# A four-layer graph network on one core: bias rows and degrees in fewer products, edge visits among the first weight products, the general path as a branch's body, and the last rows in halves

## The chip, the core and the metric

The kernel runs on one core of one Trainium2 chip. The metric is the device time of one execution in microseconds; the time before is the median of three runs. The engines are named as in the profile: PE (matrix products), PEld (PE's weight loads), DVE, ACT, POOL, and SP, which here only issues transfers and waits.

## The reference, cut to what matters

The inputs are 512 nodes with 512 features (float32) and 16384 edges, sorted by `dst`. Four layers follow one another, each with a residual around it:

```python
edge_index = jnp.stack([src, dst])
h = jnp.maximum(_layernorm(x, axis=-1), 0.0)
x = x + _L0_gnn_ref(h, edge_weight, L0_gnn_W_gcn, L0_gnn_b_gcn, L0_gnn_W_mlp, L0_gnn_b_mlp, edge_index)
h = jnp.maximum(_layernorm(x, axis=-1), 0.0)
x = x + _L1_gnn_ref(...)   # four blocks of sparse attention with a conditioned norm, and an MLP
h = jnp.maximum(_layernorm(x, axis=-1), 0.0)
x = x + _L2_gnn_ref(...)   # three diffusion steps over the symmetric adjacency
h = jnp.maximum(_layernorm(x, axis=-1), 0.0)
x = x + _L3_gnn_ref(...)   # two relational layers with gates; weights are sums of 30 bases
```

The change touches mostly the first layer:

```python
A = zeros((512, 512)).at[edge_index[0], edge_index[1]].add(edge_weights)
deg = jnp.sum(A, axis=1)
dinv = jnp.where(deg > 0, deg ** (-0.5), 0.0)
A_norm = dinv[:, None] * A * dinv[None, :]
for l in range(2):
    h = A_norm @ h
    h = h @ W_gcn[l] + b_gcn[l]
    h = leaky_relu(h @ W_mlp[l] + b_mlp[l], 0.01)
```

## The kernel before, in words

One function, `network`, writes out the whole program in the order in which each engine is to run it. No scheduler reorders it. It is called twice: once with `general=False`, for edge lists whose sorted destinations lie within a spread of ranks, and once with `general=True` inside a branch that is taken only when a flag says that the list was unusual. With these inputs it isn't taken.

**Start.** The edges are read as 128 rows ("chunks") of 128 edges: destinations, sources and types as integers (`e_i`), weights as floats (`e_r`). They are cast, and four PE transposes with one eviction put an edge on each partition (`e_c`, L342 to L345). DVE splits the weights into three bfloat16 parts (`vals`), ACT spreads destinations (`widen_dst`, L354) and values (`widen_vals`, L357) for later one-hot products. PE transposes the second graph weight (`wg2_turned`), so that the product of the two second weights, `W2`, can be formed (`W2_rows`: four rows of four products through `job`, L372). In the kernel before, the first row of `W2` is computed ahead of all visits.

**Edge visits.** `visits(c)` adds chunk c to the counts: DVE makes a one-hot matrix of the sources (`s_hot`, L564, twelve buffers), and for each window of 32 destinations that the chunk can touch a stack of weighted one-hots (`hot_dst`: `oh` L528, `st` L530, for up to sixteen chunks at a time). PE multiplies the two (L572) into one of four PSUM banks (`win`), bfloat16 with 512 columns, 195 products in all. When a window is done, ACT evicts it (`finish`, L549) and a transfer moves its counts to `CP`; after four windows `weigh` (L555) adds the three weight parts with four products of 32 columns each into `AT`.

Between visits, `after` and `spread` hang other work at given chunks, in program order: the other `W2` rows, the first layer norm (`first_moments`, `first_start`, `first_end`, `first_norm`), its transposes (`hT_chunk`), the first weights' products `uT` (`u_job`) and `t0` (`t_job`), and the small conditioning network (`cond_sine`, `cond_first`, `cond_silu`, `cond_second`). `job` takes a PSUM bank from the pool `mm`, which has two.

**After the last visit.** `decode(0)` splits the counts of the first 128 destinations on DVE (L609 to L613). The degrees come from four products with an all-ones matrix (`deg_ps`, through `calls`, L99), the fourth of them after `weigh(3)` and the last job `t_job(3)`. DVE takes the diagonal (L635), `neg_rsqrt` gives `dinv`, and `AT` is scaled by it. Then two bias rows, `b_gcn[l] @ W_mlp[l]`, are formed by `row_job`: four products each with the bias broadcast over 128 columns (L372). `decode(1)` and `decode(2)` follow on DVE, and then the four node products with the normalised adjacency (L675, L677), with `decode(3)` after the first.

**The rest.** Attention blocks, diffusion and the relational layers follow. The sums over bases (`more`, L216 on DVE, fed by POOL's transfers) are put between the other steps throughout. In the last layer each 128-row chunk of the output is one product of 4 float32 and 24 bfloat16 parts into one bank, an addition on DVE (L1203) and one transfer (L1204). After the network, every engine loads the flag (L1221) and goes through the branch (L1222), whose empty side comes first and the general network second; the end of the program is at L1245.

Of the kernel before, what the change touches and what calls it, by code (L numbers as in the profile page):

```python
# [9 lines left out]
F32 = mybir.dt.float32  # L10
# [57 lines left out]
def network(ctx, tc, a, out, flag_i, general):  # L68


    nc = tc.nc

    const = ctx.enter_context(tc.tile_pool(name="const", bufs=1))
# [176 lines left out]
    with ExitStack() as pe:  # L250
# [6 lines left out]
        e_i = edges.tile([P, 3, P], I32, name="e_i")  # L257
        e_r = edges.tile([P, 4, P], F32, name="e_r")
        nc.sync.dma_start(e_i[:, 0, :], a["dst"].rearrange("(c e) -> c e", e=P))
        nc.scalar.dma_start(e_i[:, 1, :], a["src"].rearrange("(c e) -> c e", e=P))  # L260
        nc.sync.dma_start(e_i[:, 2, :], a["edge_type_2"].rearrange("(c e) -> c e", e=P))
        nc.scalar.dma_start(e_r[:, 3, :], a["edge_weight"].rearrange("(c e) -> c e", e=P))
        wg1, wm2, wm1, wg2 = (weights.tile([P, K, D], F32, name="w") for _ in range(4))
# [76 lines left out]

        for i in range(3):
            nc.vector.tensor_copy(e_r[:, i, :], e_i[:, i, :])  # L342
        e_c = edges.tile([P, 4, EC], F32, name="e_c")
        transposed(e_c, [e_r[:, i, :] for i in range(4)], nc.vector.tensor_copy)
        dst, src, kind, wt = (e_c[:, i, :] for i in range(4))  # L345
# [156 lines left out]

        spread(0, 1, [f for c in range(1, K) for f in W2_rows(c)])
        for c in range(K):
            after(5 + c, first_moments, c)
            after(11 + c, first_norm, c)
            after(15 + c, hT_chunk, c)
        after(8, first_start)
        after(10, first_end)
        spread(20, 2, [f for j in range(K) for f in u_job(j)])  # L510
# [41 lines left out]
        def weigh(k):  # L552
# [3 lines left out]
            nc.scalar.copy(AT[:, k, :], ps)  # L556

        def visits(c):
            for i, p in enumerate(PIECES):
                if p[3] <= c < p[4] and (i, c // 16) not in groups:  # L560
                    groups[i, c // 16] = (max(p[3], c // 16 * 16),
                                          hot_dst(p, max(p[3], c // 16 * 16), min(p[4], c // 16 * 16 + 16)))
            s = hot.tile([P, N], BF16, name="s_hot")
            nc.vector.tensor_scalar(s, node_ids, src[:, c : c + 1], None, op0=OP.is_equal)  # L564
            for i, p in enumerate(PIECES):
                w = p[2]
                if not p[3] <= c < p[4]:
                    continue
                if w not in banks:
                    banks[w] = win.tile([P, N], F32, name="win")  # L570
                g0, st = groups[i, c // 16]
                nc.tensor.matmul(banks[w], st[:, c - g0, :, :], s, start=(left[w] == total[w]), stop=(left[w] == 1))  # L572
# [50 lines left out]

        decode(0)
        deg_ps = win.tile([P, N], F32, name="win")
        calls(deg_ps, [(all_ones, AT[:, k, :]) for k in range(3)], last=False)
        if not general:
            weigh(3)
        t3 = []
        for call in t_job(3, t3.append):  # L630
            call()
        calls(deg_ps, [(all_ones, AT[:, 3, :])], first=False)
        deg = small.tile([P, K], F32, name="deg", bufs=1)
        for c in range(K):
            nc.vector.scalar_tensor_tensor(e_r[:, c, :], deg_ps[:, chunk(c)], 1.0, ident, op0=OP.mult, op1=OP.mult,  # L635
                                           accum_out=deg[:, c : c + 1])
# [3 lines left out]
        nc.scalar.copy(t0[:, 3, :], t3[0])  # L640
        n = neg_rsqrt(least, 0.0, [P, K],
                      lambda: nc.vector.tensor_scalar(has_deg, deg, 0.0, -1.0, op0=OP.is_gt, op1=OP.mult))
        nc.vector.tensor_mul(dinv, n, has_deg)
# [244 lines left out]
    with ExitStack() as ph:  # L888
# [55 lines left out]
        for i in range(NB):  # L944
# [189 lines left out]
    for l in range(2):  # L1134
# [56 lines left out]
        for c in range(K):  # L1191
            ps = product([(hT[:, k, chunk(c)], root[:, k, :]) for k in range(K)]
                         + [(t[:, k, chunk(c)], part[:, k, :])
                            for k in range(K) for t, parts in ((C0T, u[0]), (C1T, u[1])) for part in parts])
            if l == 0:
# [9 lines left out]
        hT = nT  # L1205
        wr = wrel[1] if l == 0 else None

@with_exitstack
def kernel(ctx: ExitStack, tc: tile.TileContext, a: dict, out: bass.AP):
    nc = tc.nc
    ctx.enter_context(nc.allow_non_contiguous_dma(reason="biases with a feature per partition"))

    ctx.enter_context(tc.manual_schedule())
    flag_i = ctx.enter_context(tc.tile_pool(name="flag", bufs=1)).tile([1, 1], I32, name="flag_i")
    with ExitStack() as body:
        network(body, tc, a, out, flag_i, general=False)

    missed = nc.values_load(flag_i[:1, :1], min_val=0, max_val=1)  # L1221
    with tc.If(missed < 1) as none:  # L1222
        pass
    with none.Else(), ExitStack() as body:
        network(body, tc, a, out, flag_i, general=True)
# [23 lines left out]
```

## Time and profile before

| | |
|---|---|
| median of 3 runs | 851.45 us (850.77 to 851.7) |
| profiled execution | 852.14 us, of which span 850.4 us |
| PE busy | 817.5 us, 96% of the span |
| DVE busy | 676.5 us, 80% |
| ACT, POOL busy | 321.0 us, 64.2 us |
| DMA | 128.41 MB, mean 151 GB/s |
| first product of `W2` starts | 10.13 us |
| first product of `uT` starts | 33.54 us |
| last visit ends, degree products begin | 102.29 us |
| scaled `AT` meets `t0`, first product | 117.06 us |
| last addition on DVE (L1203) | 839.97 to 840.66 us |
| last issue of the output's transfer | 840.69 to 841.02 us |

All stretches of time are measured from the start of the span. Matrix products are pipelined: the interval between the starts of two is what PE is held by one, while its listed duration is longer. A float32 product of 512 columns is two instructions in the trace. A group of lines such as "PE ps L372 x8" in the chain of waits is eight such instructions, or four products.

### The profile page before, as it was taken

How to read it: one execution, taken by the hardware profiler on the slowest of the kernel's cores; microseconds unless marked ns; L12 is line 12 of the kernel's file. 1: busy time of each engine (PE TensorE's matmuls, PEld its weight loads, DVE VectorE, ACT ScalarE, POOL GpSimd, SP SyncE). 2: the span in 40 equal slices, each digit the busy share in tenths (PEclk: the TensorE clock that was granted, in tenths of full speed). 3: DMA queues.
4: the chain of work that ended last, by engine and by line, in shares of the span. 5: the costliest groups of instructions: out<-in, count | busy, mean ns of one | idle time of the engine just before them, and what ended most of it. 6: DMA issues, size and time to landing. Idle time of an engine off the chain costs nothing.

```text
span 850.4 us, 8126 instructions
## 1 busy us (share of the span) xinstructions
PE 817.5 (96%) x2549; PEld 394.1 (46%) x2549; DVE 676.5 (80%) x1183; ACT 321.0 (38%) x647; POOL 64.2 (8%) x135
## 2 busy tenths in 40 slices
PE   7999999999999999999999999999999999999995
PEld 4434344455444644444744445644446544444442
DVE  7777867878888999888997788998888967788620
ACT  4453413432654433563424752324653122311400
POOL 7000010000001001000101010101010100010000
PEclk9999999999999999999999999999999999999998
DMA  9200146213569365478457586545688720141000
GB/s 232 64 6 17 42 148 247 99 63 112 155 175 323 117 215 204 120 225 275 162 168 291 147 256 215 186 146 161 186 296 329 239 90 3 74 146 53 1 25 28
DMA packets 50693, 128.41 MB, mean 151 GB/s; under 512 B 6992, under 2 KB 7536, under 8 KB 49616
## 3 DMA queue, kind: packets, MB, share of 16 engines
q0 software_dynamic: 17552, 66.83, 24.3%
q1 hardware_dynamic: 32800, 60.84, 23.0%
q8 instruction: 22, 0.36, 0.2%
q14 instruction: 31, 0.25, 0.1%
q10 hardware_dynamic: 288, 0.13, 0.1%
HBM read 108.90 MB, written 6.29 MB: 135 GB/s over the span
## 4 chain that ended last, share of the span: by engine, by line
PE 56%; DVE 20%; DMA 7%; SPq 6%; ACT 5%; issue 4%; DVEq 0%; ACTq 0%
PE ps L99 25%; DVE wrel L216 8%; PE sp L99 7%; DMA pT<-turned 6%; SPq L933 6%; PE ps L372 5%; PE ps L1035 5%; PE win L572 5%; PE tr L119 3%; PE sp L804 2%; DVE st L156 2%; PE sp L909 2%; PE sp L666 1%; ACT p L915 1%; DVE z L1025 1%
## 5 line engine op out<-in xcount | busy, mean ns | idle before, releaser
L216 DVE SCALAR_TENSOR_TENSOR wrel<-basis,att,wrel 128x2048 f32<-128x2048 f32 x116 | 264.9, 2341 | 0.0
L99 PE MATMUL ps<-w,oT 128*128 128x512 f32 x288 | 129.5, 595 | 1.0 <-DVE x L1108 1.0
L99 PE MATMUL ps<-yT,w 128*128 128x512 f32 x256 | 112.9, 594 | 0.0
L99 PE MATMUL ps<-w,yT 128*128 128x512 f32 x224 | 101.1, 595 | 1.2 <-ACT yT L126 0.7
L200 POOL DMA_DIRECT2D basis<-in_L_gnn_basis_dram x60 | 45.2, 754 | 694.5 <-DVE wrel L216 530.2
L99 PEld LDWEIGHTS ps<-w,oT 128*128 128x128 f32 x288 | 53.1, 190 | 65.0 <-issue 56.4
L99 PEld LDWEIGHTS ps<-yT,w 128*128 128x128 f32 x256 | 48.2, 190 | 61.9 <-issue 60.9
L99 PEld LDWEIGHTS ps<-w,yT 128*128 128x128 f32 x224 | 41.1, 190 | 48.0 <-issue 44.9
L1035 PE MATMUL ps<-yT,w 128*128 128x256 f32 x256 | 58.4, 382 | 2.9 <-ACT yT L120 2.9
L131 ACT ACTIVATE g<-mv,eps_t 128x1 f32<-128x1 f32 (+1 forms) x45 | 13.3, 295 | 126.2 <-DVE mv L158 126.2
L915 ACT ACTIVATE p<-ns,stat 128x512 f32<-128x512 f32 x64 | 45.5, 711 | 35.7 <-DVE stat L913 35.6
L909 PE MATMUL sp<-kT,qT 128*128 128x512 f32 x128 | 57.6, 593 | 1.1 <-ACT kT L893 1.1
L1035 PEld LDWEIGHTS ps<-yT,w 128*128 128x128 f32 x256 | 47.4, 190 | 14.3 <-ACT yT L120 6.2
L572 PE MATMUL win<-s_hot,st 128*128 128x512 bf16 x195 | 50.4, 379 | 0.5 <-DVE s_hot L564 0.5
L913 DVE CUSTOM_DVE_ANT_0 ns<-sp,lnC 128x512 f32<-128x512 f32 x64 | 43.2, 688 | 5.5 <-PE sp L909 5.5
L905 ACT ACTIVATE p<-p,stat 128x512 f32<-128x512 f32 x64 | 43.7, 707 | 0.0
L564 DVE TENSOR_SCALAR s_hot<-node_ids,e_c 128x512 bf16<-128x512 f16 x128 | 39.9, 359 | 4.1 <-PE win L572 3.6
L909 PEld LDWEIGHTS sp<-kT,qT 128*128 128x128 f32 x128 | 24.2, 190 | 32.1 <-issue 29.9
L572 PEld LDWEIGHTS <-st 128*128 128x128 bf16 x195 | 18.7, 98 | 37.1 <-issue 23.4
L668 ACT ACTIVATE mod<-sp 128x512 f32<-128x512 f32 x64 | 32.9, 597 | 5.5 <-PE sp L666 5.5
L902 DVE RECIPROCAL stat<-stat 128x1 f32<-128x1 f32 x64 | 10.4, 163 | 29.8 <-ACT p L915 29.6
L928 DVE STREAM_TRANSPOSE turned<-p 128x512 f32<-128x512 f32 x48 | 29.9, 679 | 1.7 <-issue 0.6
(255 smaller groups left out, 1091.2 us busy)
## 6 DMA issues: line engine op xcount, KB each, us to landing
basis<-in_L_gnn_basis_dram POOLq DMA_DIRECT2D x60, 1024.0 KB, 6.5
pT<-turned SPq DMA_DIRECT2D x192, 64.0 KB
w<-in_L_gnn_m_w_dram SPq DMA_DIRECT2D x8, 1024.0 KB
w<-in_L_gnn_wv_dram SPq DMA_DIRECT2D x4, 1024.0 KB
w<-in_L_gnn_wq_dram SPq DMA_DIRECT2D x4, 1024.0 KB
w<-in_L_gnn_wk_dram SPq DMA_DIRECT2D x4, 1024.0 KB
w<-in_L_gnn_wo_dram SPq DMA_DIRECT2D x4, 1024.0 KB
w1d<-wrel POOLq DMA_DIRECT2D x2, 1024.0 KB, 6.2
```

Of the source, the lines that this page charges most:

```text
L99: nc.tensor.matmul(ps, lhsT, rhs, start=(first and i == 0), stop=(last and i == len(parts) - 1))
L200: nc.gpsimd.dma_start(t.rearrange("p (k o) -> p k o", k=K), by_partition(a[f"L3_gnn_basis{l + 1}"][b]))
L216: nc.vector.scalar_tensor_tensor(w, t, s, w, op0=OP.mult, op1=OP.add)
L372: nc.tensor.matmul(bank[0], lhsT, rhs, start=(i == 0), stop=(i == len(parts) - 1))
L564: nc.vector.tensor_scalar(s, node_ids, src[:, c : c + 1], None, op0=OP.is_equal)
L572: nc.tensor.matmul(banks[w], st[:, c - g0, :, :], s, start=(left[w] == total[w]), stop=(left[w] == 1))
L905: nc.scalar.mul(p, p, st[:, 2:3])
L909: nc.tensor.matmul(ps, qT[:, chunk(c)], kT, start=True, stop=True)
L913: nc.vector.tensor_tensor_reduce(ns, ps, lnC[:, c, :], -1.0, 3e38, OP.add, OP.min, st[:, 0:1])
L915: nc.scalar.activation(p, ns, AF.Exp, bias=st[:, 0:1], scale=-1.0, accum_out=st[:, 1:2])
L933: nc.sync.dma_start(pT[32 * b : 32 * b + 32, a, :, :], t[32 * a : 32 * a + 32, b, :, :, :])
L1035: nc.tensor.matmul(ps[:, :256], w1[:, k, chunk(j)], yT[:, k, cols], start=(k == 0), stop=(k == K - 1))
```

## The change

1. The edge types and weights are loaded before destinations and sources, and transposed and evicted in two halves; the second half's eviction goes from DVE to ACT.
2. The first row of `W2` is no longer computed ahead of the visits: all sixteen products are spread over chunks 0 to 15, one after each visit. The values of the first 16 chunks are widened in two halves, and the stacks for them are made in groups of eight chunks. All four transposes of the second graph weight are evicted by ACT. Three one-hots are made early. The first layer norm's steps move by two chunks (the transposes by one), and the first conditioning product from chunk 56 to 62.
3. The bias rows: `row_job` is replaced by `bias_row`, which runs among the visits at chunks 42 and 54. Each of its four products writes only a 32-row part of one bank, ACT scales the bank by 1/32 into SBUF, and one all-ones product per row sums the four parts later.
4. The degrees: DVE adds the first three blocks of `AT` into `part`, and two all-ones products replace four. `decode(1)` moves ahead of the degrees, and the last `t0` job is split around them.
5. The flag is loaded within the first attention block, and the empty side of the branch is dropped: the general network is the body of the branch.
6. The last 128 rows of the output are computed in two halves of 256 columns, each with its own addition and transfer.

```diff
+        nc.sync.dma_start(e_i[:, 2, :], a["edge_type_2"].rearrange("(c e) -> c e", e=P))
+        nc.scalar.dma_start(e_r[:, 3, :], a["edge_weight"].rearrange("(c e) -> c e", e=P))
         nc.sync.dma_start(e_i[:, 0, :], a["dst"].rearrange("(c e) -> c e", e=P))
         nc.scalar.dma_start(e_i[:, 1, :], a["src"].rearrange("(c e) -> c e", e=P))
...
-        transposed(e_c, [e_r[:, i, :] for i in range(4)], nc.vector.tensor_copy)
+        transposed(e_c[:, 0:2, :], [e_r[:, i, :] for i in (0, 1)], nc.scalar.copy)
...
-        widen_vals(0, 16)
-        for c in range(K):
-            wg2_turned(c, nc.vector.tensor_copy if c < 2 else nc.scalar.copy)
+        wg2_turned(0, nc.scalar.copy)
+        widen_vals(0, 8)
+        wg2_turned(1, nc.scalar.copy)
+        widen_vals(8, 16)
+        wg2_turned(2, nc.scalar.copy)
+        wg2_turned(3, nc.scalar.copy)
         widen_dst(16, 48)
-        for call in W2_rows(0):
-            call()
         widen_vals(16, 32)
...
-        def row_job(l, w, row):
-            return job([(b_gcn[:, l, k : k + 1].to_broadcast([P, P]), w[:, k, :]) for k in range(K)], add_to(row))
+        def bias_row(l, w):
+            ps = mm.tile([P, D], F32, name="ps")
+            for k in range(K):
+                nc.tensor.matmul(ps[32 * k : 32 * k + 32, :], b_gcn[:, l, k : k + 1].to_broadcast([P, 32]), w[:, k, :],
+                                 start=True, stop=True)
+            nc.scalar.mul(b_part(l), ps, 1.0 / 32.0)
...
-        spread(0, 1, [f for c in range(1, K) for f in W2_rows(c)])
+        spread(0, 1, [f for c in range(K) for f in W2_rows(c)])
...
-        after(56, cond_first)
+        after(62, cond_first)
...
+        after(54, bias_row, 1, wm2)
+        after(42, bias_row, 0, wm1)
...
-        calls(deg_ps, [(all_ones, AT[:, k, :]) for k in range(3)], last=False)
+        part = h1[:, 0, :]
+        nc.vector.tensor_tensor(part, AT[:, 0, :], AT[:, 1, :], op=OP.add)
+        nc.vector.tensor_tensor(part, AT[:, 2, :], part, op=OP.add)
+        decode(1)
...
-        for call in t_job(3, t3.append):
-            call()
-        calls(deg_ps, [(all_ones, AT[:, 3, :])], first=False)
+        last_t = t_job(3, t3.append)
+        last_t[0]()
+        last_t[1]()
+        calls(deg_ps, [(all_ones, part), (all_ones, AT[:, 3, :])])
+        last_t[2]()
+        last_t[3]()
+        for l, row in enumerate((row1, row2)):
+            ps = win.tile([P, N], F32, name="win")
+            calls(ps, [(all_ones, b_part(l))])
+            b_rows.append((row, ps))
...
-        for call in row_job(0, wm1, row1) + row_job(1, wm2, row2):
-            call()
-        decode(1)
+        for row, ps in b_rows:
+            nc.vector.tensor_tensor(row, ps, row, op=OP.add)
         decode(2)
...
+            if i == 0 and not general:
+                missed = nc.values_load(flag_i[:1, :1], min_val=0, max_val=1)
...
+            if l == 1 and c == K - 1:
+                for half in (slice(0, 256), slice(256, 512)):
+                    ps = mm.tile([P, D], F32, name="ps")
+                    calls(ps[:, half], [(t, w[:, half]) for t, w in parts])
+                    nc.vector.tensor_tensor(x[:, c, half], ps[:, half], x[:, c, half], op=OP.add)
+                    nc.sync.dma_start(out[chunk(c), half], x[:, c, half])
+                break
...
-    missed = nc.values_load(flag_i[:1, :1], min_val=0, max_val=1)
-    with tc.If(missed < 1) as none:
-        pass
-    with none.Else(), ExitStack() as body:
+    with tc.If(missed > 0), ExitStack() as body:
         network(body, tc, a, out, flag_i, general=True)
```

More of the change, by code (lines that the diff above doesn't have):

```diff
@@ L71, in network @@
     nc = tc.nc
+    missed = None
     const = ctx.enter_context(tc.tile_pool(name="const", bufs=1))
@@ L258, in network @@
         e_r = edges.tile([P, 4, P], F32, name="e_r")
+        nc.sync.dma_start(e_i[:, 2, :], a["edge_type_2"].rearrange("(c e) -> c e", e=P))
+        nc.scalar.dma_start(e_r[:, 3, :], a["edge_weight"].rearrange("(c e) -> c e", e=P))
         nc.sync.dma_start(e_i[:, 0, :], a["dst"].rearrange("(c e) -> c e", e=P))
         nc.scalar.dma_start(e_i[:, 1, :], a["src"].rearrange("(c e) -> c e", e=P))
-        nc.sync.dma_start(e_i[:, 2, :], a["edge_type_2"].rearrange("(c e) -> c e", e=P))
-        nc.scalar.dma_start(e_r[:, 3, :], a["edge_weight"].rearrange("(c e) -> c e", e=P))
         wg1, wm2, wm1, wg2 = (weights.tile([P, K, D], F32, name="w") for _ in range(4))
@@ L339, in look_for_stray @@
                                            accum_out=n_bad[:, 0:1])
-        for i in range(3):
+        e_c = edges.tile([P, 4, EC], F32, name="e_c")
+        nc.vector.tensor_copy(e_r[:, 2, :], e_i[:, 2, :])
+        transposed(e_c[:, 2:4, :], [e_r[:, i, :] for i in (2, 3)], nc.vector.tensor_copy)
+        for i in range(2):
             nc.vector.tensor_copy(e_r[:, i, :], e_i[:, i, :])
-        e_c = edges.tile([P, 4, EC], F32, name="e_c")
-        transposed(e_c, [e_r[:, i, :] for i in range(4)], nc.vector.tensor_copy)
+        transposed(e_c[:, 0:2, :], [e_r[:, i, :] for i in (0, 1)], nc.scalar.copy)
         dst, src, kind, wt = (e_c[:, i, :] for i in range(4))
@@ L446, in t_job, with b_part @@
             return job([(uT[:, k, chunk(c)], wm1[:, k, :]) for k in range(K)], done or copy_to(t0[:, c, :]))
-        def row_job(l, w, row):
-            return job([(b_gcn[:, l, k : k + 1].to_broadcast([P, P]), w[:, k, :]) for k in range(K)], add_to(row))
+        def b_part(l):
+            return cond[0][:, 3, :] if l else e_r.rearrange("p a b -> p (a b)")
+        def bias_row(l, w):
[4 more added lines that the diff above has]
+            nc.scalar.mul(b_part(l), ps, 1.0 / 32.0)
         cond = []
@@ L501, in cond_second @@
                 nc.scalar.activation(condT[32 * g : 32 * g + 16, :], ps[:16, :], AF.Identity, bias=f_b[:, 1:2])
-        spread(0, 1, [f for c in range(1, K) for f in W2_rows(c)])
+        spread(0, 1, [f for c in range(K) for f in W2_rows(c)])
         for c in range(K):
[L505 to L509, printed above, removed]
+            after(7 + c, first_moments, c)
+            after(13 + c, first_norm, c)
+            after(16 + c, hT_chunk, c)
+        after(10, first_start)
+        after(12, first_end)
         spread(20, 2, [f for j in range(K) for f in u_job(j)])
@@ L556, in weigh, with group, hot_src @@
             nc.scalar.copy(AT[:, k, :], ps)
+        def group(c):
+            return (c // 16 * 16, c // 16 * 16 + 16) if c >= 16 else (c // 8 * 8, c // 8 * 8 + 8)
+        def hot_src(c):
+            s = hot.tile([P, N], BF16, name="s_hot")
+            nc.vector.tensor_scalar(s, node_ids, src[:, c : c + 1], None, op0=OP.is_equal)
+            return s
+        early = {} if general else {c: hot_src(c) for c in range(3)}
         def visits(c):
             for i, p in enumerate(PIECES):
[L560 to L564, printed above, removed]
+                if p[3] <= c < p[4] and (i, group(c)) not in groups:
+                    c0, c1 = group(c)
+                    c0, c1 = max(p[3], c0), min(p[4], c1)
+                    groups[i, group(c)] = c0, hot_dst(p, c0, c1)
+            s = early.pop(c) if c in early else hot_src(c)
             for i, p in enumerate(PIECES):
@@ L570, in visits @@
                     banks[w] = win.tile([P, N], F32, name="win")
-                g0, st = groups[i, c // 16]
+                g0, st = groups[i, group(c)]
                 nc.tensor.matmul(banks[w], st[:, c - g0, :, :], s, start=(left[w] == total[w]), stop=(left[w] == 1))
@@ L624, in network @@
         decode(0)
+        b_rows = []
         deg_ps = win.tile([P, N], F32, name="win")
-        calls(deg_ps, [(all_ones, AT[:, k, :]) for k in range(3)], last=False)
+        part = h1[:, 0, :]
+        nc.vector.tensor_tensor(part, AT[:, 0, :], AT[:, 1, :], op=OP.add)
+        nc.vector.tensor_tensor(part, AT[:, 2, :], part, op=OP.add)
+        decode(1)
         if not general:
@@ L629, in network @@
         t3 = []
-        for call in t_job(3, t3.append):
-            call()
-        calls(deg_ps, [(all_ones, AT[:, 3, :])], first=False)
+        last_t = t_job(3, t3.append)
[8 more added lines that the diff above has]
+            b_rows.append((row, ps))
         deg = small.tile([P, K], F32, name="deg", bufs=1)
         for c in range(K):
-            nc.vector.scalar_tensor_tensor(e_r[:, c, :], deg_ps[:, chunk(c)], 1.0, ident, op0=OP.mult, op1=OP.mult,
+            nc.vector.scalar_tensor_tensor(h1[:, 1, chunk(c)], deg_ps[:, chunk(c)], 1.0, ident, op0=OP.mult, op1=OP.mult,
                                            accum_out=deg[:, c : c + 1])
@@ L639, in network @@
         nc.vector.tensor_scalar(least, deg, 1e-30, None, op0=OP.max)
-        nc.scalar.copy(t0[:, 3, :], t3[0])
         n = neg_rsqrt(least, 0.0, [P, K],
                       lambda: nc.vector.tensor_scalar(has_deg, deg, 0.0, -1.0, op0=OP.is_gt, op1=OP.mult))
+        nc.scalar.copy(t0[:, 3, :], t3[0])
         nc.vector.tensor_mul(dinv, n, has_deg)
@@ L1191, in network @@
         for c in range(K):
-            ps = product([(hT[:, k, chunk(c)], root[:, k, :]) for k in range(K)]
-                         + [(t[:, k, chunk(c)], part[:, k, :])
-                            for k in range(K) for t, parts in ((C0T, u[0]), (C1T, u[1])) for part in parts])
+            parts = ([(hT[:, k, chunk(c)], root[:, k, :]) for k in range(K)]
+                     + [(t[:, k, chunk(c)], part[:, k, :])
+                        for k in range(K) for t, parts_ in ((C0T, u[0]), (C1T, u[1])) for part in parts_])
+            if l == 1 and c == K - 1:
[5 more added lines that the diff above has]
+                break
+            ps = product(parts)
             if l == 0:
@@ L1206, in network @@
         wr = wrel[1] if l == 0 else None
+    return missed
 @with_exitstack
@@ L1218 @@
     with ExitStack() as body:
-        network(body, tc, a, out, flag_i, general=False)
-    missed = nc.values_load(flag_i[:1, :1], min_val=0, max_val=1)
-    with tc.If(missed < 1) as none:
-        pass
-    with none.Else(), ExitStack() as body:
+        missed = network(body, tc, a, out, flag_i, general=False)
+    with tc.If(missed > 0), ExitStack() as body:
         network(body, tc, a, out, flag_i, general=True)
```

## The prediction

> **What bounds the kernel now.** I read the page first, then the chain of waits of the stretches that the diff touches, then who waited for whom, then single source lines at the end of the program. The page says that the whole is PE's:
>
> ```profile
> PE 817.5 (96%) x2549; PEld 394.1 (46%) x2549; DVE 676.5 (80%) x1183; ACT 321.0 (38%) x647; POOL 64.2 (8%) x135
> ...
> PE 56%; DVE 20%; DMA 7%; SPq 6%; ACT 5%; issue 4%; DVEq 0%; ACTq 0%
> ```
>
> PE is never long idle, so an edit pays here if it takes products off PE in a stretch where PE holds the chain, or a wait of PE, or time behind PE's end. The chain of waits from 95 to 165 us shows such a stretch:
>
> ```profile
> 102.29 2.58 PE win L99 x6
> 104.87 0.99 PE ps L555 x8
> 105.86 3.63 PE ps L372 x8
> 109.49 0.86 PE win L99 x2
> 110.35 6.88 PE ps L372 x16
> ...
> 128.19 3.70 PE ps L99 x8
> ```
>
> The lines are three degree products, `weigh(3)`, the last `t0` job, the fourth degree product, the two bias rows, and the last of four node products. A float32 product of 512 columns costs 0.86 us here; the four 32-column products of `weigh` cost 0.99 together, since they share the array. The chain from 0 to 36 us shows the start:
>
> ```profile
> 10.33 5.56 PE ps L372 x8
> ...
> 29.62 0.76 DVE st L530
> 30.38 0.28 DVE s_hot L564
> 30.65 0.04 issue
> 30.69 0.38 PE win L572
> ...
> 33.54 1.12 PE ps L372 x2
> ```
>
> Four `W2` products take 5.56 us instead of 3.44, and PE later waits for DVE. Who waited for whom, PE from 5 to 165 us:
>
> ```profile
> PE ps L485 <- ACT oT L479: 1.4, 1, 1.4
> ```
>
> `cond_first` waits for ACT's sine (between the starts of the products around it, 1.56 us are lost). The program's end, by source line (L1222 is the branch, L1245 what follows it; min/median/max in ns, first and last start):
>
> ```profile
> L1222 SPq EVENT_SEMAPHORE  x8: 17/17/17, 842.1 to 844.3; - x8
> ...
> L1222 PEldq COMPARE_BRANCH  x2: 92/1962/3833, 836.5 to 840.1; - x2
> ...
> L1222 SPq COMPARE_BRANCH  x2: 43/46/49, 842.0 to 844.4; - x2
> ```
>
> ```profile
> L1245 SPq EVENT_SEMAPHORE  x14: 17/28/28, 847.1 to 850.3; - x14
> ```
>
> SP issues the last output by 841.03, loads the flag and tests it (to 842.04), waits for the landing (844.1), jumps at 844.4 and arrives at 847.1. This jump of 2.6 us comes after the landing; PE's jump of 3.8 us lay beside it.
>
> **The change, part by part**, against the profiled execution (span 850.4, 1.7 outside it, 852.14 in all; the median 851.45 is 0.69 less).
>
> *Start: 1.2 us gained.* The four products of the first `W2` row run before any visit now; afterwards four visits (0.216 each) lie between them. The products are then the same, so what counts is PE's first product and its waits. First product: 10.13 now. Afterwards PE must pass the 16 transposes, the last four of which need a bank that ACT frees. ACT's order is half an `e_c` eviction (about 0.4, between L120's 0.59 for 512 columns and half), 0.62 (L354), 0.59, 0.95 (half of L357's 1.9), 0.59: from 5.5 this is 8.7, the transposes at their early 0.21 each end at 9.6, and the first stack (L530, half of 1.22) is there at about 8.9. So 9.7: 0.4 gained. Waits: 0.15 + 0.62 at 29.4 and 30.7 because DVE had waited 4.6 us for ACT's logarithm at 25.0, which stood behind the eviction of a `W2` row at 24.5. Afterwards it stands behind the row evicted after chunk 7, near 20.5, while `x` lands at 18.9 as now; DVE is some 4 us earlier and both waits go (0.8). The wait of 0.42 for the last `relu_neg` at 33.5 stays. DVE loses two evictions (0.69 each), and ACT gains them, with hardly anything else due.
>
> The early products are slow by a clock that comes up late: the weight loads below are 0.85 apart, those at 108 us 0.43, and the step falls at 14.4, 4.3 us after the first product.
>
> ```profile
> 10.99 0.33 PEld L372 LDWEIGHTS ps<-w,oT 128*128 128x128 f32 x1 [0.52 <-issue]
> 11.84 0.33 PEld L372 LDWEIGHTS ps<-w,oT 128*128 128x128 f32 x1 [0.52 <-issue]
> ```
>
> I keep 4.3 us from the first product; a second such stretch at half speed would cost 2.2 us, the first beginning no later gains nothing more. The Trainium skill ("TensorE: Matmul & The Clock Gate", Part 1) speaks of some 3.4 us of sustained work, seen in a window that runs freely; by its figure the fast clock would come up to 0.9 us sooner, and an estimate from it adds 0.4 us of gain.
>
> *Sine: 1.6 gained.* At chunk 62 the sine has been done; ACT's second table load (1.28) then has no PE work behind it. ACT also gets two bias evictions (0.6 each), and its four banks of windows are the cover; without it at most 1.2 comes back.
>
> *Bias rows among the visits: 2.0 lost there.* Two times four 32-column products, the form of L555: 0.99 each. The row before them frees its bank in time, because two visits lie between.
>
> DVE must follow if PE comes earlier. From 60 to 76 us it waits 6.5 us for PE in all; from 76 to 102 never, and the visits find their one-hot only 0.73 us or more old. So it inherits PE's lead at 76 us, which is 1.2 + 1.6 - 2.0 = 0.8 us, and nothing more. The last visit then ends at 101.5.
>
> *After the last visit: 7.15 gained.* Now 29.6 us from 102.29 to the end of the fourth node product (131.89), of which 14.94 up to 117.23 and 14.66 for four products of 3.44 with waits. Afterwards PE has: 0.65 waiting for ACT's copy of the last window (the degree products hide it now), `weigh` 1.0, four `t0` products 3.44, two degree products 1.72, two row sums 1.72, four node products 13.76, latency 0.15: 22.45. DVE must keep this: relative to the last visit, `decode(0)` ends at +1.3 (as now), two additions (0.69 each) +2.7, `decode(1)` (2.8, as at 117.9) +5.5; the degrees are in the bank at +5.25; from L635's first start to `dinv` is 2.5 (110.39 to 112.9) +8.0; the first scaled block 0.5 later +8.5, just when the row sums end (+8.53). So `dinv` isn't late, but has no slack: what delays `part` is paid in full, up to 1 us. Then two row additions (1.4) and `decode(2)` (2.8) end at +13, the first node product at +12; `decode(3)` lies in the second's time, and the bank waits of now (0.16 + 0.56) go. `wm2` and `wm1` are free sooner; the loads into them follow `decode(3)` on SP, 8 us earlier, with the same lead on their readers. Bases start some 2 us earlier and have 30 us of slack. So the lead should pass on.
>
> *Flag load: 0.1 lost.* One load an engine (0.46 to 0.55), on SP 0.86; on PE between 260.4 and 261.05, where it idles for ACT, on DVE behind sums of 2.3 us. Queued behind SP's is the next block's weights, due much later.
>
> *End: 2.5 gained.* The halves: 8 float32 parts of 256 columns are 0.216 per instruction (L1035: 3.46 for 16). A bfloat16 part of 256 columns isn't in this trace: between 0.109 (transposes, whose loads of 0.14 are hidden) and 0.216, unchanged. 48 of them cost 5.3 to 10.4 us instead of 5.2; I take 0.11, as the nearest in size: 0.1 lost. The last addition is 0.42 instead of 0.69 (between 0.29 for 128 columns, L635, and 0.69): 0.27 gained. Then, from SP's last issue: now 9.33 to the end. Afterwards SP jumps at once, while the transfer flies (3.05 from issue to SP's release): 2.6 to 3.8, say 3.2; eight waits 0.55; and 3.3 from arrival to end as now: 7.05, so 2.3 gained. In those 3.3 lies a hole of 1.6 (847.5 to 849.1), which may come or go with the code's place; thus 1.0 to 4.2. The Trainium skill ("Runtime: NRT & Kernel Launch", Instruction fetch mechanics) says that a taken branch to code outside the loaded pages stalls for its fetch: this speaks against the change, which keeps one far jump. The trace's jumps agree in size, and what I claim is its place ahead of the landing. If the jump stayed behind the landing, only the flag's 0.96 and the 0.27 would be left.
>
> Sum: 1.2 + 1.6 - 2.0 + 7.15 - 0.1 - 0.1 + 2.5 = 10.25. Profiled 852.14 - 10.25 = 841.9; median **841.2 us**.
>
> **The rivals.**
> - *The jump stays exposed*, because the branch waits for all transfers first: 1.3 less, 842.5. For it: the waits stood ahead of the jump now. Against: they belong to the empty side, which now is the jump's target. Chance 0.17.
> - *The clock comes up one stretch later*, because visits and waits thin out the early products: 843.4. Chance 0.08.
> - *Narrow products cost as wide ones*: either bias products don't share the array (3.44 instead of 0.99 a row, 4.9 in all, 846.1) or bfloat16 halves aren't cheaper (5.1, 846.3). L555 speaks against the first, the transposes against the second. Chance 0.08.
> - *Slower: the turned attention weights land later.* The chain has nine waits for `pT<-turned`, 4.6 to 7.3 us, 53.3 in all. PE's lead is 8 us and that of the bases' stream 2, so that their transfers may meet otherwise. If each took the longest, 7.26, this costs 12.0 and gives 853.2. It decides from 10.25 / 9 = 1.14 us each. Against it: the bases' loads are released by DVE's sums, which move along. Chance 0.05.
>
> **How the numbers follow.** The forecast has 0.60, and 0.02 is left for no change. Its own range: early clock and lost `part` slack 1 us each way down, the hole 1.65 up: 838.8 to 843. With the first two rivals the range is 838.6 to 844.4. About 0.2% (1.7 us) is what a measurement of this kernel can tell from no change. Faster 0.93, same 0.02, slower 0.05.
>
> **What would show it.** Right: no L372 product of `b_gcn` with 128 columns; first node product about 8.5 us after the last visit, last visit near 101.5; first `u_job` product near 32.3; no wait before L485; SP's far jump starting within 0.2 us of its last issue. Wrong: DVE gaps or late one-hots from 76 to 102 us, `dinv` later than the row sums, part products 0.2 us apart in the last rows, or longer waits for `pT` than 6 us on average.

## The result and the profile after

The changed kernel takes **840.48 us** (median of 4 runs, 840.22 to 841.18) against 851.29 us for the kernel before on the same chip: a ratio of 0.9875, 95% interval 0.9858 to 0.9892. The prediction was 841.2 us, range 838.6 to 844.4. The profiled execution takes 841.18 us with a span of 839.31, and all readings below are of that one execution, times from its start.

The two lines of the page that stood first in the prediction read now:

```profile
PE 811.5 (97%) x2581; PEld 395.0 (47%) x2581; DVE 676.4 (81%) x1186; ACT 323.5 (39%) x653; POOL 64.4 (8%) x135
...
PE 58%; DVE 19%; DMA 8%; SPq 7%; ACT 5%; issue 4%; DVEq 0%; ACTq 0%
```

PE has lost 6.0 us of busy time though it issues 32 instructions more. Of the gain of about 11 us, then, a good part is not products saved. Cut at marks that both kernels have, the two profiled executions differ like this ("visit 20" is the visit just ahead of the first `u_job` product):

| stretch | before | after | difference | predicted |
|---|---|---|---|---|
| start to the end of visit 20 | 33.28 | 31.46 | -1.82 | -1.2 |
| to the end of the last visit | 69.01 | 69.96 | +0.95 | +0.4 |
| to the end of the four node products | 29.60 | 22.53 | -7.07 | -7.15 |
| to PE's end | 708.05 | 708.15 | +0.10 | +0.2 |
| to the end of the span | 10.42 | 7.21 | -3.21 | -2.5 |

**After the last visit.** The chain of waits from 94 to 128 us:

```profile
97.86 3.56 PE win L598 x16
101.42 1.72 PE ps L570 x8
103.14 1.92 PE ps L376 x4
105.06 1.72 PE win L101 x4
106.77 1.72 PE ps L376 x4
108.49 1.72 PE win L101 x4
110.21 13.74 PE ps L101 x32
```

This is the prediction's list in its order: `weigh(3)` with the wait ahead of it (L570, 1.72), half of the last `t0` job, two degree products, the other half, two row sums, and four node products. The last visit ends at 101.42 (predicted 101.5), the first node product starts 8.8 us later (8.5), and the fourth ends at 123.95. Before, it ended at 131.89. The lead is 7.94 us there and 7.84 us at PE's end, 708 us later.

**The start.** From 0 to 36 us the chain now holds:

```profile
5.01 9.53 DMA w<-in_L_gnn_W_mlp_dram
...
14.58 1.13 PE ps L376 x2
...
31.28 0.61 ACT mod L128
...
31.93 1.13 PE ps L376 x2
```

What PE waited for between 5 and 165 us:

```profile
PE ps L376 <- DMA w<-in_L_gnn_W_mlp_dram: 0.7, 1, 0.7
PE tr L121 <- DVE e_r L347: 0.7, 1, 0.7
PE ps L376 <- ACT mod L128: 0.5, 1, 0.5
```

In the kernel before, the list had this line too:

```profile
PE win L572 <- DVE s_hot L564: 0.5, 1, 0.5
```

The sine's line (1.4 before) and this wait for the one-hot have left the list. A new one stands first: the last quarter of the second MLP weight lands at 14.54, and PE, which needs it for the fourth product of the first `W2` row, is ready 0.7 us before. The first product is at 10.01 (predicted 9.7) and the first `u_job` product at 31.93 (32.3).

**The end**, by source line (L1269 is the branch, L1290 what follows it):

```profile
L1269 SPq EVENT_SEMAPHORE  x8: 17/17/17, 835.6 to 836.1; - x8
...
L1269 PEldq COMPARE_BRANCH  x1: 3752/3752/3752, 830.0 to 830.0; - x1
...
L1269 SPq COMPARE_BRANCH  x1: 53/53/53, 833.0 to 833.0; - x1
```

```profile
L1290 SPq EVENT_SEMAPHORE  x14: 17/28/28, 836.2 to 839.2; - x14
```

SP's last issue ends at 832.92, its branch starts 0.05 us later, and its first event at the target is at 835.59. The output's last packets end at 834.18, under this jump. From the last issue to the end are 6.38 us, where there were 9.34. Within the fourteen events, 17 to 28 ns each, SP stands still once, from 836.47 to 837.90.

### The profile page after: what moved, and what is told of

Its sections match the earlier page's. It is cut to its first block, busy times and chain, and to the rows that moved or that the text cites. A ratio compares the mean times of both kernels' runs of the same rounds, so it can differ in the third digit from the quotient of the medians.

```text
span 839.3 us, 8200 instructions
## 1 busy us (share of the span) xinstructions
PE 811.5 (97%) x2581; PEld 395.0 (47%) x2581; DVE 676.4 (81%) x1186; ACT 323.5 (39%) x653; POOL 64.4 (8%) x135
## 4 chain that ended last, share of the span: by engine, by line
PE 58%; DVE 19%; DMA 8%; SPq 7%; ACT 5%; issue 4%; DVEq 0%; ACTq 0%
PE ps L101 26%; DVE wrel L218 8%; PE sp L101 8%; DMA pT<-turned 6%; SPq L969 6%; PE ps L1073 5%; PE win L598 5%; PE ps L376 5%; PE tr L121 2%; PE sp L840 2%; DVE st L158 2%; PE sp L945 2%; PE sp L702 1%; DMA w<-in_L_gnn_W_mlp_dram 1%; ACT p L951 1%
## 5 line engine op out<-in xcount | busy, mean ns | idle before, releaser
L101 PE MATMUL ps<-w,oT 128*128 128x512 f32 (+1 forms) x296 | 129.7, 584 | 1.0 <-DVE x L1146 1.0
```

The lines of the kernel that those rows point to most:

```text
L101: nc.tensor.matmul(ps, lhsT, rhs, start=(first and i == 0), stop=(last and i == len(parts) - 1))
```

## The experiments

The kernel before had medians of 851.05 to 852.35 us in these comparisons. A single execution's start scatters: visit 20 ends between 30.1 and 31.5 us in the eleven profiles with the new start and between 32.4 and 33.3 in the three with the old. The scatter comes from ahead of one product: in all eleven, visit 20 ends 16.88 us after the start of the first `W2` row's fourth product, and that start lies between 13.2 and 14.6 us. So beside the median each run is read from visit 20 on.

**1. The old end on the changed kernel.** The flag is loaded at the end again, and the empty side of the branch is back.

```diff
-            if i == 0 and not general:
-                missed = nc.values_load(flag_i[:1, :1], min_val=0, max_val=1)
...
-    with tc.If(missed > 0), ExitStack() as body:
...
+    missed = nc.values_load(flag_i[:1, :1], min_val=0, max_val=1)
+    with tc.If(missed < 1) as none:
+        pass
+    with none.Else(), ExitStack() as body:
```

> The changed kernel with the program's end as before: flag loaded after the network, empty side of the branch first. Theory (SP's far jump now lies beside the last landing): from SP's last issue, flag 1.0, landing of the half transfer at about 1.8, jump from 2.1 to 4.7, 3.3 from arrival to end, 8.0 in all instead of 6.4 in the changed kernel's trace: 1.6 us slower than it, about 842.1. Rival (the end's gain comes from the half transfer or from the place of the code): within 0.3 of the changed kernel, 840.5 to 840.8.

Measured: 843.78 us (843.25 to 844.44), ratio 0.9911, interval 0.9896 to 0.9926. That is 3.3 us above the changed kernel, twice what was expected. The tail from the last issue is 9.42 us. The branch in its profile:

```profile
L1269 SPq EVENT_SEMAPHORE  x8: 17/17/17, 833.0 to 835.2; - x8
...
L1269 SPq COMPARE_BRANCH  x2: 43/46/49, 832.9 to 835.2; - x2
```

SP passes four of its eight events by 833.28, is held until 834.96 and jumps at 835.2. So SP was released 3.0 us after its issue of the half, as it was after the whole piece in the kernel before (3.05), where I had expected 1.8. The size of the piece isn't the reason. The output's last packet ends 2.51 us after the issue here and 2.56 in the kernel before, and SP is released 0.5 us behind it; in the changed kernel the same half's last packet ends 1.26 us after its issue, and in run 3 the whole piece's 1.38. Here nine of the 144 packets, one sixteenth, end between 1.78 and 2.51 us, behind a 16 KB transfer of instructions that runs from 0.27 to 1.67 us after the issue; all others are done by 1.02. The load of the flag lies within this wait.

**2. Early flag, old form of the branch.** Of the first diff, only the branch's lines.

> The changed kernel with the flag loaded early, as in the change, but the branch in its old form, empty side first. Theory: the flag's load is covered by the landing anyway, the order of landing and jump is what counts: as the run with the whole old end, about 1.5 us slower than the changed kernel, 842.0; SP's far jump starts about 2 us after its last issue. Rival (the late flag load was the loss): within 0.3 of the changed kernel.

Measured: 843.64 us (843.3 to 844.34), ratio 0.9909, interval 0.9894 to 0.9924; tail 9.40 us.

```profile
L1269 SPq EVENT_SEMAPHORE  x8: 17/17/17, 832.3 to 835.2; - x8
...
L1269 SPq COMPARE_BRANCH  x2: 43/48/53, 832.2 to 835.3; - x2
```

SP reaches its events some 0.2 us after its last issue instead of 1.07, but jumps 3.1 us after it, where run 1 has 3.3: it leaves them 0.5 us after the output's last packet, which again ends late (2.32 us after the issue, behind such a transfer of instructions). With this form of the branch, moving the load alone is worth nothing; what counts is that the jump comes ahead of the landing.

**3. The new end alone, on the kernel before.** Early flag and new branch; nothing else of the change.

> The kernel before with the early flag and the new branch alone, the last rows whole. Theory: from SP's last issue 6.4 to 6.8 us to the end instead of 9.3 (jump 2.6, landing at 3.05, then as in the changed kernel): 2.5 to 2.9 faster than before, about 848.6. Rival (it pays only with the halved last transfer): 1.0 to 1.3 faster, about 850.1.

Measured: 848.37 us (848.09 to 848.74), ratio 0.9962, interval 0.9948 to 0.9977: 2.7 us gained, tail 6.43 us. With the first two runs this settles the end's part at 2.7 to 3.3 us.

**4. The last rows whole.**

```diff
-            if l == 1 and c == K - 1:
+            if False:
```

> The changed kernel with the last 128 rows whole again. Theory: the addition ends 0.27 later, the whole transfer lands 3.05 us after its issue, about when SP arrives from its jump, so 0.1 to 0.2 more; PE's products take the same: 0.4 us slower, 840.9. Rival (the shorter last transfer is on the path): 1.4 us more, 841.9.

Measured: 840.92 us (840.02 to 842.89), ratio 0.9882, interval 0.9863 to 0.9902. The difference of 0.4 us from the changed kernel lies within what these runs can tell. From PE's end to the end of the span its profile has 7.50 us instead of 7.21: the longer last addition, 0.69 instead of 0.42, and nothing else.

**5. The bias rows wide again**, 128 columns each, placed where the row sums are.

```diff
-        after(54, bias_row, 1, wm2)
-        after(42, bias_row, 0, wm1)
...
-        for l, row in enumerate((row1, row2)):
+        for l, row, w in ((0, row1, wm1), (1, row2, wm2)):
             ps = win.tile([P, N], F32, name="win")
-            calls(ps, [(all_ones, b_part(l))])
+            calls(ps, [(b_gcn[:, l, k : k + 1].to_broadcast([P, P]), w[:, k, :]) for k in range(K)])
```

> The changed kernel with the bias rows again as four products of 128 columns each, where the row sums stand, and none among the visits. Theory (PE's work sets the first layer): 6.88 for the products, less 1.72 for the row sums and 1.98 for the narrow products: 3.2 us slower, 843.7; the visits end 2.0 earlier, because DVE waits for PE up to 76 us and inherits its lead. Rival (from 76 to 102 us DVE sets the visits' end): the visits end less than 0.8 earlier and the kernel is 4.4 to 5.2 slower, about 845.3.

Measured: 843.49 us (842.97 to 844.07), ratio 0.9906, interval 0.9891 to 0.992: 3.0 us above the changed kernel. The chain from 94 to 128 us shows both sides of the trade:

```profile
98.06 1.72 PE ps L568 x8
...
105.13 6.87 PE win L101 x16
111.99 13.73 PE ps L101 x32
```

The rows cost 6.87 us here, 5.15 more than the row sums (1.72). Without them the visits from visit 20 take 67.76 us instead of 69.96, so the narrow rows cost 2.2 us there, and 5.15 - 2.2 is the 3.0 measured. That the last visit comes 2.2 us sooner also shows that DVE follows PE's lead through the visits after 76 us.

**6. The conditioning product at chunk 56 again.**

```diff
-        after(62, cond_first)
+        after(56, cond_first)
```

> The changed kernel with the first conditioning product back at chunk 56. Theory: PE waits again for ACT's sine, about 1.5 us, and DVE loses the same lead: 1.2 to 1.6 slower, 841.9, visits' end at 102.6 to 103.0. Rival (DVE holds the visits' end anyway, so a wait at 60 us is made up): less than 0.5 slower.

Measured: 845.25 us (843.67 to 847.49), ratio 0.9928, interval 0.9913 to 0.9944: 4.8 us lost, some three times what was expected. PE waited for longer, and then something else happened. Its wait between 50 and 76 us, and the busy times of three stretches (the columns are stretch, length, busy time and count of PE, PEld, DVE, ACT and POOL, granted clock, share and rate of the transfers):

```profile
PE ps L498 <- ACT oT L462: 2.2, 1, 2.2
```

```profile
60.00:63.00 3.00, 1.53 (x5) 0.54 (x6) 0.15 (x1) 1.87 (x3) 0.00 (x0) 1.00 0.00 0
63.00:66.60 3.60, 3.60 (x8) 1.34 (x7) 2.39 (x6) 0.68 (x2) 0.00 (x0) 0.53 0.09 23
66.60:70.00 3.40, 3.35 (x14) 1.41 (x13) 2.04 (x7) 0.59 (x1) 0.00 (x0) 1.00 0.00 0
```

The sine itself has been done since 59.51 us; PE is released at 61.4 by the eviction of a bias row (L462, 0.61), which stands on ACT behind the next table load (1.28). So the wait has grown from 1.56 to 2.2 us, and it is no longer the wait for the sine alone. After it the granted clock falls to 0.53 from 63.0 to 66.6 us: eight PE instructions where the next stretch of like length has fourteen. At half speed these 3.4 us lose about 1.7. From visit 20 to the last visit the profile has 73.93 us instead of 69.96: 4.0, which is 2.2 + 1.7 within 0.1. In the kernel before, the wait of 1.56 us was followed by a clock of 1.00 throughout; its row for the same stretch:

```profile
63.00:66.60 3.60, 3.60 (x14) 1.64 (x13) 3.00 (x10) 0.64 (x2) 0.00 (x0) 1.00 0.07 18
```

Behind the first 20 us no other profile here has PE idle for more than 1.4 us at a time, and in none does the clock fall before PE's end. This is one execution, of 844.15 us; three of the six took 846.4 to 847.5, and what they lost beyond it no profile shows. The Trainium skill ("TensorE: Matmul & The Clock Gate", What's actually happening) has the clock halved after an idle window of some 3.4 us and full again after as long a busy one: the length of the slow stretch agrees, but here the only long wait ahead of it was of 2.2 us. Whether that wait alone began it was not tested.

**7. Four degree products again**, three of them ahead of `decode(1)`, without the additions on DVE.

```diff
-        part = h1[:, 0, :]
-        nc.vector.tensor_tensor(part, AT[:, 0, :], AT[:, 1, :], op=OP.add)
-        nc.vector.tensor_tensor(part, AT[:, 2, :], part, op=OP.add)
+        calls(deg_ps, [(all_ones, AT[:, k, :]) for k in range(3)], last=False)
...
-        calls(deg_ps, [(all_ones, part), (all_ones, AT[:, 3, :])])
+        calls(deg_ps, [(all_ones, AT[:, 3, :])], first=False)
```

> The changed kernel with four degree products, three of them before the last window's weighing, and no sums of blocks on DVE. Theory: 1.72 more of PE, of which 0.7 lies in PE's wait for ACT's copy of the last window: 1.0 slower, 841.5; the normalisation is no later, since the row sums stand behind it. Rival (the two DVE additions stood on the path to the normalisation): not slower, or up to 0.4 faster.

Measured: 842.21 us (841.61 to 842.71), ratio 0.9888, interval 0.9874 to 0.9902: 1.7 us lost. The chain from 94 to 128 us:

```profile
100.88 2.58 PE win L101 x6
103.46 0.99 PE ps L570 x8
```

Three degree products (2.58) hide the wait ahead of `weigh` (0.99 instead of 1.72), and the first node product starts 9.8 us after the last visit instead of 8.8. The two saved products are thus worth 1.0 us, not 1.72. Of the other 0.7 us of the median the profile shows 0.4 later, between there and PE's end.

**8. The old start on the changed kernel**: order of the loads, one `e_c` eviction, the first `W2` row ahead of the visits, the old due times of the first norm.

```diff
-        spread(0, 1, [f for c in range(K) for f in W2_rows(c)])
+        for call in W2_rows(0):
+            call()
+        spread(0, 1, [f for c in range(1, K) for f in W2_rows(c)])
...
-            after(7 + c, first_moments, c)
+            after(5 + c, first_moments, c)
...
```

> The changed kernel with the start as before: old order of the edge loads, first weight row ahead of the visits, two evictions on DVE, stacks of sixteen chunks, first norm two chunks earlier. Theory: the first uT product returns from 31.9 to about 33.5 and all that follows moves by it: 1.6 slower, 842.1; the clock comes up 4 us later, near 14.4. Rival (the clock's step is chance and the order is worth nothing): less than 0.5 slower, or the clock's step near 10.4.

Measured: 842.3 us (842.15 to 842.98), ratio 0.9889, interval 0.9874 to 0.9903: 1.8 us lost, as expected. DVE's wait for the logarithm is back in its chain, behind the eviction of a `W2` row on ACT:

```profile
24.19 0.59 ACT w L381
24.77 0.21 ACT g L133
```

And among PE's waits from 5 to 165 us, where the changed kernel has none for a one-hot:

```profile
PE win L595 <- DVE s_hot L576: 0.5, 1, 0.5
```

Its clock stepped up at 12.40 us. In run 3, also with the old start, it did so at 10.37, in the kernel before at 14.48, and in the profiles with the new start between 8.3 and 10.5. So the step isn't set by the first product, and it is worth little: between 10.37 and 14.48 visit 20 moved by 0.9 us only (32.37 and 33.28), since with the early step PE waits for the last quarter of the second MLP weight (0.98 us in run 3). The Trainium skill ("TensorE: Matmul & The Clock Gate", What's actually happening) says that this step differs from run to run by some 500 ns either way; in these profiles, which are of several variants, it lies anywhere between 8.3 and 14.5 us.

**9. The code behind the branch moved.** The general body, not executed here, gets 16 more transfers to issue.

```diff
-        for c in range(K):
-            nc.sync.dma_start(x[:, c, :], a["x"][chunk(c), :])
+        for _ in range(5 if general else 1):
+            for c in range(K):
+                nc.sync.dma_start(x[:, c, :], a["x"][chunk(c), :])
```

> The general body, which is not executed on these data, gets 16 more DMA issues on SP near its beginning, so that the code behind the branch lies at another place; nothing else changes. In the end events of every profile so far SP has one hole of 1.3 to 1.8 us among events of 17 to 28 ns (in the changed kernel 836.47 to 837.90). Theory (the hole is SP waiting for the next block of its instructions, at a fixed place of the code): the hole moves to another event or leaves the list; where it leaves it, the tail from the last issue is about 1.4 us shorter (5.0 instead of 6.38) and the time 839.1. Rival (the hole is a wait for another engine or for the last write, at whatever place the events are): tail and time unchanged, 840.5 within 0.4, and the hole at the same time after the jump.

Measured: 839.74 us (839.12 to 841.2), ratio 0.9864, interval 0.9848 to 0.9879. The last events in its profile:

```profile
L1291 SPq EVENT_SEMAPHORE  x14: 17/28/28, 836.9 to 838.5; - x14
```

The fourteen events take 1.6 us instead of 3.0; the gap is gone, and the tail is 4.9 us (5.0 expected). The median moved by only 0.7, with an interval that overlaps the changed kernel's. In the profiled execution (840.32 us) one wait for `pT` near 608 us was 1.3 us long, which the changed kernel's profile doesn't have; two of the four executions took 839.1 to 839.2, as expected. That the gap belongs to a place in the code shows elsewhere too: it stands after the twelfth event behind the jump in the other six profiles with the new end and both halves issued by SP, and after the fourteenth in the two (runs 3 and 4) where SP has one issue fewer. The Trainium skill ("Runtime: NRT & Kernel Launch", Instruction fetch mechanics) says that an engine's instructions come in blocks of 256. A gap that goes away when code is put ahead of it agrees with that; that the gap is such a fetch isn't shown.

**10. The last half's output issued by ACT.**

```diff
-                    nc.sync.dma_start(out[chunk(c), half], x[:, c, half])
+                    (nc.scalar if half.start else nc.sync).dma_start(out[chunk(c), half], x[:, c, half])
```

> The second half of the last rows is issued on ACT's queue instead of SP's, so that SP has its last issue one half (some 2.6 us) earlier and can jump and pass its end events while PE still multiplies. Theory (the tail is SP's own chain: jump 2.6, events with a hole of 1.4, end): SP leaves the path; what is left is ACT's jump behind its issue (2.4 in the profile of before) and its last events, or the landing (3.0 from issue to release), then about 1 us: tail 3.5 to 4.4 instead of 6.38, time 838 to 838.6. Rival (the events after the jump wait for every engine and for the landing, so that the hole and what follows come anyway after the last engine): gain at most 0.5, 840.0 to 840.5.

Measured: 838.19 us (837.63 to 838.66), ratio 0.9842, interval 0.9829 to 0.9856: 2.3 us below the changed kernel.

```profile
L1269 SPq EVENT_SEMAPHORE  x8: 17/17/17, 830.5 to 834.4; - x8
...
L1269 SPq COMPARE_BRANCH  x1: 53/53/53, 827.8 to 827.8; - x1
...
L1269 ACTq COMPARE_BRANCH  x1: 54/54/54, 832.2 to 832.2; - x1
...
L1269 ACTq EVENT_SEMAPHORE  x1: 17/17/17, 835.1 to 835.1; - x1
```

SP jumps at 827.8, while PE still multiplies. It is then held at its events from 830.83 until 834.23, 0.55 us after the output's last packet, and its last events come behind that and behind ACT's jump, 2.9 us long, which ends at 835.13. The tail from the last issue is 4.4 us. The gap of 1.4 us isn't seen either: none of SP's stops behind 834.23 is over 0.6 us. Whether the wait for the landing covers it or the code's place took it away (SP has one issue fewer) wasn't separated. Beside run 9, which hasn't the gap either (4.9), the tail is 0.6 us shorter, so that of the 2.0 us between the tails 1.4 may be the gap.

**11. The bias rows in PE's waits**: one ahead of the first `u_job` product, one behind the last visit.

```diff
...
+        after(20, bias_row, 1, wm2)
...
-        after(54, bias_row, 1, wm2)
-        after(42, bias_row, 0, wm1)
...
         decode(0)
+        bias_row(0, wm1)
```

> The two bias rows (0.99 us of PE each) leave the visits at 42 and 54: one goes ahead of the first u_job product at chunk 20, where PE waits 0.63 us for the last relu, the other behind the last visit, where PE waits some 0.65 to 0.73 us for the copy of the last window. Theory (in the visits up to 76 us PE is the bound and the rows are paid there in full, as the wide rows were): 2.0 us back, less the 0.3 and 0.4 that the waits don't cover: 1.3, time 839.2. Rival (the waits move instead of being filled, since DVE and ACT set them and DVE has no more lead in the visits after 76 us): at most 0.3 gained, 840.2 to 840.5; a row ahead of the node products that is not covered would even cost up to 0.7.

Measured: 840.03 us (839.09 to 841.05), ratio 0.9869, interval 0.9854 to 0.9884. The median alone doesn't tell it from the changed kernel. The chain from 94 to 126 us does:

```profile
95.89 3.56 PE win L597 x16
99.45 0.99 PE ps L460 x8
100.45 0.86 PE ps L569 x8
```

The row takes the place of the wait, and `weigh` costs 0.86 instead of 1.72. From visit 20 to PE's end are 798.99 us instead of 800.64: 1.65 gained.

**12. Runs 10 and 11 together.**

> Both edits of the two runs before together: the bias rows in PE's waits at chunk 20 and behind the last visit, and the last half's output on ACT's queue. In the profiles of those two the stretch from visit 20 to PE's last product was 798.99 with the first (800.6 in the changed kernel), and the tail from the last issue 4.3 with the second (6.38). Theory (the two gains lie in different stretches and add): from visit 20 to PE's end 799.0 again, tail 4.3, time 838.19 less 1.6: 836.6 (with the start's spread of about 1 us, 835.6 to 837.6). Rival (the 1.6 of the rows is only the scatter between executions, as the medians 840.03 and 840.48 would have it): 837.7 to 838.2, and a stretch of 800.6.

Measured: **836.98 us** (836.54 to 837.13), ratio 0.9824, interval 0.9811 to 0.9837. From visit 20 to PE's end are 799.00 us, and the tail is 4.05. The gains add, and this version beats both kernels, the changed one by 3.5 us. As in run 10, the gap isn't seen in SP's last events.

## Why the prediction was right, point by point

- **After the last visit**, 7.15 predicted, 7.07 measured. The new order of products was right piece by piece, and so was the finding that `dinv` isn't late. The wait ahead of `weigh` is 0.73 instead of 0.65. Runs 5 and 7 show what the two edits bring: 5.15 us for the rows in this stretch (3.0 net of what they cost among the visits), and 1.0 us for the degrees in the profile. The remaining 0.9 us is in the four node products, 13.74 us against 14.66 with their waits; no run tests that part alone.
- **Bias rows among the visits**, 2.0 predicted, 2.2 in run 5. Four 32-column products do share the array: 0.99, as for `weigh`. Where the other 0.2 comes from stays open.
- **Sine**, 1.6 predicted. Between visit 20 and the last visit the kernel without the rows among the visits (run 5) has 67.76 us against 69.01 before: 1.25. That comparison holds the rest of the change too, and is no test of this term alone. Of the missing 0.35, 0.2 is the wait for the last `relu_neg`, which the prediction left at 0.42 and which now is 0.63 between the products around it, as PE comes to it earlier. What run 6 takes away is more than this term, because putting the product back also meets a bias eviction and a clock that falls; neither was in the kernel before.
- **End of the visits**, 101.5 predicted, 101.42 measured. That these agree is luck in part: the start gained 0.6 us more than predicted and the visits gave back 0.55 more.
- **Start**, 1.2 predicted, 1.8 in the profile, 1.8 by run 8's median. Both waits for DVE are gone, as predicted. The first product came 0.12 us earlier instead of 0.4, and it is not what counts: the fourth product of the first row, at 14.58 us after 14.87, has to wait for its weights. From that product to visit 20 are 16.88 us in all profiles with the new start and 18.4 to 18.5 with the old. These 1.5 to 1.6 us are the waits for DVE (0.77 in the prediction's reading) and four visits (0.86), which now go ahead of that product instead of behind it and which the prediction counted as worth nothing. The step that failed is "4.3 us from the first product" for the clock: in the changed kernel it came at 10.40 us, 0.4 us after the first product. The weights at 14.54 I hadn't named.
- **End**, 2.5 predicted (2.3 for the jump, 0.27 for the addition, on separate working), 3.21 measured. The mechanism was right: the jump ahead of the landing takes the landing off the path. The mis-sized term is "2.6 to 3.8, say 3.2" for SP's jump: it took 2.57 us from the branch's end to the first event, as long as before (2.61). The gap of 1.6 us, now 1.4, stayed, and the doubt about it was real: in run 9 it goes when the code is moved.
- **Halves.** The 256-column bfloat16 parts are 0.109 us apart, as taken.
- **Flag load.** It lies at 250.8 to 263.7 us (0.56 on SP), and no cost is seen. Runs 1 and 2 show that with the old form of the branch it cost nothing at the old place either; a late load with the new form, where it would stand ahead of SP's jump, wasn't run.

Of the rivals, the exposed jump fell (SP jumps 0.05 us after its last issue), and so did the late clock and the wide-priced narrow products (0.99 a row). The slower one, later `pT`, needed 1.14 us more in each of nine waits: the chain has 53.5 us of them in all after 53.3 before. Single waits moved by -0.9 to +1.3 us. Run 9's extra wait shows that such a wait can grow in a single execution, there by 1.3 of the 10.25 us needed. The undershoot of the forecast's gain, 0.7 us, is the end and the start together, less what the visits gave back.

## What to carry to other kernels

Where one chain runs through the whole program, here over PE (58%), DVE (19%) and transfers (8%), a lead won early can pass to the end almost whole (7.94 us at 124, 7.84 at 832). It is then worth cutting products of 128 equal columns down to 32, and putting the remaining work into waits rather than beside them: the same two rows cost 2.2 us among busy visits and 0.55 us (2.2 less the 1.65 of run 11) in two waits. The end of a program is a stretch of its own. Let the engine that has the far jump make it ahead of the last landing (2.7 to 3.3 us here), and mind where the code behind the jump lies (1.4 us of the tail). Giving the last transfer to another engine made the tail 2.0 us shorter, but the gap went with it. Before taking a late result's cost to be the wait alone, see what the clock does after the wait.

## What the runs showed of the hardware that was not expected

- In run 6 a wait of PE of 2.2 us at 59.3 to 61.5 us was followed, from 63.1 us on, by 3.4 us at a granted clock of about half (0.53 in the stretch); a wait of 1.56 us in the kernel before was not. It was seen in one execution.
- In the start the half speed is seen in the spacing of products alone. The clock column of the same stretches reads 1.00 from 5 us on, in both kernels: the record that it is made from begins with the step itself (14.48 us before, 10.40 after), so it says nothing of the time ahead of it.
- The last output packet ended 1.24 to 1.60 us after its issue in the eleven profiles with the new end, for 128 KB as for 256 KB, and 2.3 to 2.6 us after it in the three with the old end. In those three alone a 16 KB transfer of instructions started just behind the issue (by 0.07 to 0.33 us), and the late packets end behind it. That it delayed them fits; no run moves it alone.
- SP's stop of 1.4 us among its last events depends on where the code lies: sixteen issues that are never executed took it away (run 9), and one issue fewer moved it by two events (runs 3 and 4).
